# Adding gathered edge rows on VectorE instead of TensorE in a graph network

## The chip, the cores and the metric

The kernel runs on one core of one Trainium2 chip. The metric is the device time of one execution in microseconds (us). Five engines work side by side: TensorE (matrix products; PE, and PEld for loading its weights), VectorE (DVE), ScalarE (ACT), GpSimd (POOL) and SyncE (SP). Each has an instruction queue of its own that it works off in order. SBUF is the on-chip memory, PSUM the small memory into which TensorE writes; tables lie in DRAM. A gather is one indirect DMA on the POOL queue: for each of 128 partitions it fetches one row of a table, by a row number that lies in SBUF.

## What is computed

N = 6250 nodes carry 256 features, E = 100000 edges (src, dst) are sorted by dst. Each layer adds to each node the rows of the sources of its edges, and sends the result through three dense products:

```python
def agg(h):
    return jax.ops.segment_sum(h[src], dst, num_segments=N)
for l in range(NL - 1):          # NL = 4: three such layers
    h = x + agg(x)
    h = jax.nn.relu(h @ W1s[l] + b1s[l])
    h = jax.nn.relu(h @ W2s[l] + b2s[l])
    x = h @ W3s[l] + b3s[l]
h = x + agg(x)                   # and the last, with cW1, cW2 (64 wide), cW3
```

Before the first layer stand a layer norm and a relu; at the end the input is added. A node has 16 edges on average, and the number differs from node to node.

## The kernel before

The 6250 nodes are 49 blocks of 128. The kernel multiplies by the first weight before it aggregates, so what is gathered or multiplied is already a table of 256 columns for each layer (`tables`, one in DRAM for each layer). It aggregates in two ways at once.

*Panels.* For 31 of the blocks (`panels`), the adjacency matrix is built in layer 0 from one-hot products (`build`, L1013, with `one_hot`, L991, on VectorE and the casts L1043 and L1045), stored as bytes in DRAM (`mats`), and in every layer fetched again, cast to float (L1464 on ScalarE, L1466 on VectorE from layer 1 on) and multiplied with the whole table, which lies in SBUF as a high and a low part (`XY`). These are the products of L1491, 49 steps for each panel of up to four blocks. Layer 0 does not multiply the last panel, since it is still being built.

*Gathers.* The other blocks (`gone`: 22 in layer 0, 18 in each later layer) are gathered (class `Gathered`, L1264). The edges of a block's two halves of 64 nodes are taken in runs of 128, nine runs for each half, so 18 gathers (L1309) a block. A gathered tile holds 128 edges in edge order, so a row may belong to any node of the half. To add it up, VectorE makes a one-hot of 32 columns for each run (`one_hots`, L1334), and TensorE multiplies one-hot and rows into PSUM (`sums`, L1353). Runs that can touch two quarters take part twice: 22 products a block, in two visits, four of them side by side on different columns. Then VectorE adds the block's own row (L1371, L1380), TensorE transposes (L1391) and the block goes through the other products (`mlp`, L1169).

The order of all work is written out by the program, in one order for each engine. A model clock (`clock`, advanced by `passed` by the expected time of each product) stands for TensorE's progress. `Gathered.begin` spreads a layer's gathers evenly over the time that `work_of` expects for the layer, `send` puts each in the POOL queue behind the product then current (`after`), and rows are used LEAD = 21 us after they are asked for. A layer's gathers begin once its whole table is in DRAM (`store`, L1233). `tick` and `job` place the smaller steps.

*Preparation.* `look` (L607) finds where each node group's edges begin and fetches edge numbers in small gathers (`ask`, L597), while `normed` (L819) makes the first table. The first gathers of layer 0 go out as the matrix build starts; the first 28 steps only build (PRE), then products and build go on together.

Of the kernel before, what the change touches and what calls it, by code (L numbers as in the profile page):

```python
# [8 lines left out]
F32 = mybir.dt.float32  # L9
# [387 lines left out]
def sorted_edges(  # L397
# [56 lines left out]
    Q = P // 4  # L454
    TS = 9
    T = 2 * TS
    CUT = (3, 5)

    ROUNDS = [(3, 3), (4, 4), (0, 5), (1, 6), (2, 7), (None, 8)]
# [12 lines left out]
    S0 = 2 * panels[0][0]  # L472
    assert gone[-2] == panels[-1] and sorted(
        b + i for b, n in gone[:-2] + gone[-1:] + panels for i in range(n)) == list(range(NT))
    NQ = len(gone)
    PW = 4 * T

    left = [T * sum(n for _, n in gone[:q]) for q in range(NQ + 1)]

# [7 lines left out]
    clT = const.tile([P, 2, GSUB, NSUB - S0], BF16, name="clT")  # L487
    cT, loT = clT[:, 0], clT[:, 1]
    idx = const.tile([P, left[NQ]], I32, name="idx")
    rel = const.tile([P, left[NQ]], F32, name="rel")  # L490
# [7 lines left out]
    tables = [dram.tile([N, C], F32, name=f"table{l}") for l in range(NLAYER + 1)]  # L498
# [108 lines left out]
    def look(pool):  # L607
# [23 lines left out]
        nc.vector.memset(one, 1.0)  # L631
        firsts = pool.tile([1, EB], F32, name="near", bufs=1)
# [24 lines left out]

        place_i = pool.tile([P, NQ, PW], I32, name="hi", bufs=1)
        for q, (b, _) in enumerate(gone):
            nc.gpsimd.iota(place_i[:, q, :], pattern=[[1, PW]], base=T * b, channel_multiplier=-TS)  # L660
        place = pool.tile([P, 1], F32, name="place", bufs=1)
        nc.gpsimd.iota(place, pattern=[[0, 1]], base=0, channel_multiplier=P,
                       allow_small_or_imprecise_dtypes=True)
        node = pool.tile([P, GSUB], F32, name="node", bufs=1)
# [26 lines left out]
        for q in range(GSUB):  # L691
            for w, e in ((wd, dst), (ws, src)):
# [4 lines left out]
        both = pool.tile([P, 2], F32, name="both", bufs=1)  # L697
        sel = pool.tile([P, NQ, PW], F32, name="near_i", bufs=1)
        some = pool.tile([P, NQ, PW], F32, name="rel", bufs=1)
        nc.vector.tensor_copy(both[:NSUB, 0:1], first[:NSUB, 0:1])  # L700
        nc.vector.tensor_copy(both[:NSUB, 1:2], low[:NSUB])
        nc.vector.tensor_scalar(some[:NSUB], place_i[:NSUB], float(TS - 1), None, op0=OP.is_le)
        nc.vector.scalar_tensor_tensor(sel[:NSUB], place_i[:NSUB], 0.0, some[:NSUB],
                                       op0=OP.is_ge, op1=OP.mult)
        ps = ps_m.tile([P, W], F32, name="ps")
        for q in range(NQ):
            nc.tensor.matmul(ps[:PW, 2 * q:2 * q + 2], sel[:NSUB, q, :], both[:NSUB, :],
                             start=True, stop=True)
        spread = pool.tile([P, NQ, 2], F32, name="spread", bufs=1)
        nc.vector.tensor_copy(spread[:PW], ps[:PW, :2 * NQ].rearrange("p (q t) -> p q t", t=2))  # L710

        part = pool.tile([P, NQ], F32, name="part", bufs=1)
        nc.vector.scalar_tensor_tensor(part[:PW], spread[:PW, :, 1], float(-T), spread[:PW, :, 0],
                                       op0=OP.mult, op1=OP.add)
        for q, (b, _) in enumerate(gone):
            nc.vector.tensor_scalar(part[:PW, q:q + 1], part[:PW, q:q + 1], place[:PW, 0:1],
                                    float(T * P * b), op0=OP.add, op1=OP.add)
        skip = pool.tile([P, NQ], F32, name="skip", bufs=1)  # L720
        nc.vector.tensor_scalar(skip[:PW], part[:PW], float(E - P), None, op0=OP.min)
        from_i = pool.tile([P, NQ], I32, name="from_i", bufs=1)
        nc.vector.tensor_copy(from_i[:PW], skip[:PW])
        nc.vector.tensor_tensor(skip[:PW], part[:PW], skip[:PW], OP.subtract)
        base = pool.tile([P, NQ], F32, name="base", bufs=1)
        nc.vector.tensor_scalar(base[:PW], spread[:PW, :, 1], -1.0, None, op0=OP.add)
        gds = pool.tile([P, 2, NQ, P], I32, name="near_i", bufs=1)
        gd, gs = gds[:, 0], gds[:, 1]
        for q, (_, n) in enumerate(gone):
            for w, e in ((gd, dst), (gs, src)):  # L730
                asks.append((w[:n * T, q, :], e, from_i[:n * T, q:q + 1]))
# [3 lines left out]
        H = GSUB // 4  # L735
        for q0 in range(0, GSUB, H):
            cut = slice(q0, q0 + H)
            ask(len(asks) - 2 * (GSUB - q0 - H) - 2 * NQ)
            r = pool.tile([P, H, P], F32, name="rel", bufs=1)
            f = pool.tile([P, H, P], F32, name="f", bufs=1)  # L740
# [10 lines left out]
            for t, o in ((r, cT), (f, loT)):  # L751
                for i in range(0, H, 4):
                    ps = ps_m.tile([P, W], F32, name="ps")
                    for k in range(4):
                        nc.tensor.transpose(ps[:, k * NSUB:(k + 1) * NSUB], t[:NSUB, i + k, :],
                                            ident[:NSUB, :NSUB])
                    nc.scalar.copy(o[:, q0 + i:q0 + i + 4, :],
                                   ps[:, :4 * NSUB].rearrange("p (q s) -> p q s", q=4)[:, :, S0:])
            yield

# [859 lines left out]
```

## Time and profile before

| | us |
|---|---|
| median of three runs | 2344.69 (2342.46 to 2354.30) |
| the profiled execution, in all | 2343.82 |
| its span, first to last instruction | 2342.0 |
| TensorE busy | 2175.8 |
| VectorE busy | 972.8 |
| ScalarE busy | 891.8 |
| POOL busy | 1429.4 |

The granted TensorE clock was 0.98 over the span. The DMA engines were busy about half the time and moved 371 MB, 182 MB of it by the POOL queue. In the rows below, "L1309 POOL DMA_INDIRECT rows<-table,idx x1368 | 1374.1, 1004 | 830.7" means: line 1309, on POOL, an indirect DMA that writes the tile `rows`, 1368 times, 1374.1 us busy in all, 1004 ns on average, and 830.7 us of idle time of that engine just before them; what ended the idle time follows. In a row in order of time, the first two numbers are start and duration, and the brackets hold the idle time before it and what released it. Matmuls overlap, so a mean duration is longer than busy time divided by count; two records stand for one full float32 product.

### The profile page before, as it was taken

The page shows a single profiled execution, that of the slowest core. Times are in us where ns is not written, and L with a number is a line of the kernel's source. Part 1 is how long each engine was busy: PE and PEld are TensorE (multiplying, and loading weights), DVE is VectorE, ACT ScalarE, POOL GpSimd, SP SyncE. Part 2 cuts the span into 40 slices and gives each one's busy share as a digit, 9 for nine tenths or more (in the row PEclk, how much of TensorE's full clock was granted, in tenths as well). Part 3 has the DMA queues.
Part 4 walks back from the last instruction along what each step waited for, and adds up shares of the span by engine and source line. Part 5 has one row for each costly group of instructions (what it writes and reads, how often), then busy time and mean ns, then how long its engine had stood idle before and what let it go on. Part 6 is the DMA issues. An engine that isn't in the chain of part 4 may idle for free. (4 is left out here: it accounts for less than half of the span.)

```text
span 2342.0 us, 34300 instructions
## 1 busy us (share of the span) xinstructions
PE 2175.8 (93%) x12062; PEld 1570.0 (67%) x12062; DVE 972.8 (42%) x2844; ACT 891.8 (38%) x1816; POOL 1429.4 (61%) x1442
## 2 busy tenths in 40 slices
PE   5888998999998999999999999999999999999898
PEld 3656666666665877676766877777677866666565
DVE  6887656556555422222223422222224423232222
ACT  4775545454545423232223432232233322222221
POOL 3635666666666266666666366666664566666663
PEclk9979999999999999999999999999999999999999
DMA  4545555555556554444455554545445655545553
GB/s 151 152 154 176 173 158 174 159 166 173 164 173 200 165 151 151 149 131 149 148 156 178 181 152 134 170 136 161 140 152 159 182 167 156 168 143 172 158 153 107
DMA packets 195882, 371.43 MB, mean 159 GB/s; under 512 B 32790, under 2 KB 122986, under 8 KB 195700
## 3 DMA queue, kind: packets, MB, share of 16 engines
q0 software_dynamic: 67264, 181.96, 26.9%
q1 hardware_dynamic: 126510, 185.34, 24.2%
q8 instruction: 96, 1.57, 0.3%
q10 hardware_dynamic: 1926, 1.85, 0.3%
q14 instruction: 86, 0.70, 0.1%
HBM read 310.61 MB, written 58.07 MB: 157 GB/s over the span
## 5 line engine op out<-in xcount | busy, mean ns | idle before, releaser
L1309 POOL DMA_INDIRECT rows<-table,idx x1368 | 1374.1, 1004 | 830.7 <-PE agg L1491 276.0
L1491 PE MATMUL agg<-a,XY 128*128 128x512 f32 (+1 forms) x6076 | 1484.3, 394 | 52.6 <-issue 39.0
L1491 PEld LDWEIGHTS agg<-a,XY 128*128 128x128 f32 x6076 | 1108.4, 189 | 334.6 <-issue 126.0
L1464 ACT CAST a<-at 128x512 fp32r<-128x512 uint8 (+1 forms) x943 | 546.9, 607 | 694.7 <-PE agg L1491 528.9
L1466 DVE CAST a<-at 128x512 fp32r<-128x512 uint8 (+1 forms) x576 | 256.2, 459 | 582.2 <-PE agg L1491 397.8
L1353 PE MATMUL sums<-rows,hot 128*32 128x256 f32 x3344 | 240.4, 387 | 8.1 <-issue 4.4
L1043 ACT CAST at<-bp 128x392 uint8<-128x392 f32 x276 | 131.3, 488 | 277.8 <-PE bp L1035 197.4
L1045 DVE CAST at<-bp 128x392 uint8<-128x392 f32 x220 | 124.1, 564 | 218.2 <-PE bp L1035 152.3
L1353 PEld LDWEIGHTS sums<-rows,hot 128*32 128x32 f32 x3344 | 106.0, 110 | 132.1 <-issue 72.2
L1035 PE MATMUL bp<-hi,lo 128*128 128x196 bf16 x992 | 143.7, 264 | 47.3 <-issue 18.7
L1035 PEld LDWEIGHTS <-lo 128*128 128x128 bf16 x992 | 76.0, 102 | 129.4 <-issue 86.6
L1380 DVE TENSOR_TENSOR u<-u,sums 128x256 f32<-128x256 f32 x76 | 31.8, 419 | 309.4 <-PE agg L1491 301.4
L1183 PE MATMUL ps<-h,w 128*128 128x512 f32 (+5 forms) x392 | 158.3, 544 | 0.5 <-issue 0.5
L994 DVE TENSOR_TENSOR hi<-cols,pairs 128x784 bf16<-128x784 bf16 x248 | 139.3, 562 | 0.0
L1212 PE MATMUL ps<-w,h 128*128 128x256 f32 x588 | 134.8, 380 | 3.4 <-PE ps L1212 1.6
L1334 DVE TENSOR_TENSOR hot<-colf,rel 128x64 f32<-128x64 f32 x836 | 126.9, 220 | 0.0
L1212 PEld LDWEIGHTS ps<-w,h 128*128 128x128 f32 x588 | 110.5, 190 | 20.2 <-issue 2.7
L1183 PEld LDWEIGHTS ps<-h,w 128*128 128x128 f32 (+1 forms) x392 | 67.2, 184 | 65.3 <-issue 56.4
L1230 DVE TENSOR_TENSOR zz<-ps,w 128x512 f32<-128x512 f32 (+1 forms) x78 | 50.2, 658 | 137.8 <-PE ps L1212 82.3
L994 DVE TENSOR_TENSOR lo<-lanes,pairs 128x512 bf16<-128x512 bf16 x248 | 104.2, 420 | 2.6 <-ACT pairs L989 1.4
L1186 ACT ACTIVATE h<-ps,bias 128x512 f32<-128x512 f32 (+5 forms) x98 | 60.6, 634 | 114.1 <-PE ps L1183 81.6
L1398 ACT ACTIVATE h<-ps,bias 128x256 f32<-128x256 f32 (+1 forms) x84 | 33.5, 450 | 149.4 <-PE agg L1491 48.8
(138 smaller groups left out, 744.9 us busy)
## 6 DMA issues: line engine op xcount, KB each, us to landing
at<-mat SPq DMA_DIRECT2D x189, 448.0 KB
mat<-at SPq DMA_DIRECT2D x31, 784.0 KB
rows<-table,idx POOLq DMA_INDIRECT x1368
table<-zz SPq DMA_DIRECT2D x69, 256.0 KB
back<-table SPq DMA_DIRECT2D x118, 128.0 KB
at<-mat SPq DMA_DIRECT2D x25, 336.0 KB
xs<-in_x_dram SPq DMA_DIRECT2D x8, 768.0 KB
table<-zs SPq DMA_DIRECT2D x24, 256.0 KB
```

Of the source, the lines that this page charges most:

```text
L994: nc.vector.tensor_tensor(o.rearrange("p q (n t) -> p q n t", t=2), values.rearrange("p (n t) -> p n t", t=2)[:, None, :, :].to_broadcast( ...
L1035: mm = nc.tensor.matmul(bp[:, m * HW:(m + 1) * HW], lo[:, q + m, :], hi[:, q + m, :], start=True, stop=True)
L1043: nc.scalar.copy(o, v)
L1045: nc.vector.tensor_copy(o, v)
L1183: mm = nc.tensor.matmul(ps[:mp, :w], weights[l][0][:, c, i * P:i * P + mp], h1[:, c, :w], start=(c == 0), stop=(c == KC - 1))
L1212: mm = nc.tensor.matmul(o, h2[0][:, c, nodes], w3[:, c, :], start=(c == 0), stop=(c == KC - 1))
L1309: got = nc.gpsimd.indirect_dma_start(out=t, out_offset=None, in_=tables[self.l][:, :], in_offset=bass.IndirectOffsetOnAxis(ap=idx[:, o:o + ...
L1334: nc.vector.tensor_tensor(hot[:, i, :, :], colf[:, None, i * Q:(i + 1) * Q].to_broadcast([P, 2, Q]), rel[:, o + k:o + k + TS + 1:TS, None] ...
L1353: nc.tensor.matmul(self.sums[(2 * h + m) * Q:(2 * h + m + 1) * Q, :C], self.hots[r, m][:, h, :], self.rows[g, h, k], start=(r == 0), stop= ...
L1464: nc.scalar.copy(o, mat[l, p][j])
L1466: nc.vector.tensor_copy(o, mat[l, p][j])
L1491: mm = nc.tensor.matmul(agg[c][:, :w], XY[:, j, o:o + P], a[:, :w], start=(j == 0 and half == 0), stop=(j == NT - 1 and half == 1))
```

## The change

Gathered rows come by node instead of by edge. Tile k of a block holds, in partition p, the row of node p's k-th edge, for k below K = 17; a node with fewer edges gets a row of zeros (the tables have 128 rows more, filled with zeros). Such tiles need no one-hot: VectorE adds them up. Two tiles share a buffer of 128x512, so one add handles a pair (`pair`, seven for a block), and `fold` adds both halves, the 17th tile and the block's own row. Edges beyond a node's 17th go into OV = 2 further tiles of 128 slots for the whole block, which pass two full one-hot products on TensorE (`add`). A block has 19 gathers instead of 18, TensorE two products instead of 22.

```diff
+            def pair(self, g, k):
+                t = self.rows.pop((g, k))
+                if k == 3:
+                    self.acc = work.tile([P, 2, C], F32, name="acc", bufs=1)
+                    nc.vector.tensor_tensor(self.acc, self.rows.pop((g, 1)), t, OP.add)
+                else:
+                    nc.vector.tensor_tensor(self.acc, self.acc, t, OP.add)
+            def fold(self, g):
...
+                nc.vector.tensor_tensor(u, XY[:, b, :C].bitcast(F32), XY[:, b, C:].bitcast(F32),
+                                        OP.add)
...
+                nc.vector.tensor_tensor(u, u, self.acc[:, 0, :], OP.add)
+                nc.vector.tensor_tensor(u, u, self.acc[:, 1, :], OP.add)
+                nc.vector.tensor_tensor(u, u, self.rows.pop((g, K - 1)), OP.add)
+                self.hot = work.tile([P, OV, P], F32, name="hot", bufs=2)
+                nc.vector.tensor_tensor(self.hot, colf[:, None, :].to_broadcast([P, OV, P]),
+                                        rel[:, c, :, None].to_broadcast([P, OV, P]), OP.is_equal)
+            def add(self, g):
+                b, n, i, _ = self.blocks[g]
+                for j in range(OV):
+                    mm = nc.tensor.matmul(sums[:, :C], self.hot[:, j, :], self.rows.pop((g, K + j)),
+                                          start=(j == 0), stop=(j == OV - 1))
+                    passed(C * FULL32, mm)
+                self.finish(b, n, i, sums)
```

The pace follows the new counts, and rows are used 13 us after they are asked for. The buffers are seven pairs and four single tiles instead of 24 to 26 single ones. The model clock's price for two visits a block (VISIT) goes, `work_of` counts two products.

```diff
             def begin(self):
                 self.first = clock[0] + LEAD
                 self.end = begun[self.l] + work_of(self.l) - TAIL
-                self.pace = (self.end - self.first) / (self.upto[-1] - self.upto[1])
+                self.pace = (self.end - self.first) / (len(self.order) - 1)
...
-        LEAD, TAIL = 21.0, 10.0
-        COLS, FULL32, TURN, VISIT, BUILD, BURST = 0.457e-3, 1.68e-3, 0.4, 1.7, 0.2, 0.3
+        LEAD, TAIL = 13.0, 10.0
+        COLS, FULL32, TURN, BUILD, BURST = 0.457e-3, 1.68e-3, 0.4, 0.2, 0.3
...
-            t += len(layers[l].blocks) * (sum(VISIT for _ in VISITS[l > 0]) + TURN)
+            t += len(layers[l].blocks) * (OV * C * FULL32 + TURN)
```

In the preparation, `look` no longer fetches runs of 128 edges for the gathered blocks (14 small gathers) and turns them by transposes (L800). It counts where each single node's edges begin (`count`, small comparisons and products of one column), brings the counts to the nodes' partitions by products, and gathers the first 17 edge numbers of every node, one small gather for each of the 22 blocks. Where a node has fewer, `slot_rows` puts the number of a zero row. Two blocks ahead of their use in layer 0, `overflow` finds the edges beyond the 17th with a comparison and two small products and gathers their numbers, two more small gathers a block, in the POOL queue between the row gathers. Layer 0's row gathers begin after 22 of the 56 steps that only build, instead of before the first. The build has two PSUM buffers instead of three, since `overflow` takes one.

```diff
+        for c in range(NG):
+            asks.append((idx[:, c, :], src, from_i[:, c:c + 1]))
         ask(len(asks))
...
+        def gather():
+            for j in range(OV):
+                asks.append((over[:, c, j:j + 1], src, e_i[:, j:j + 1]))
+            ask(OV)
+
+        later(1, edges)
+        later(3, gather)
...
-        ) as ps_a, tc.tile_pool(name="ps_b", bufs=3, space=PSUM) as ps_b:
+        ) as ps_a, tc.tile_pool(name="ps_b", bufs=2, space=PSUM) as ps_b:
             begun = {0: clock[0]}
-            layers[0].begin()
-            layers[0].send(layers[0].upto[1])
+            READY = 22
...
+                if built[0] == READY:
+                    slot_rows()
+                    layers[0].begin()
```

Some steps may no longer follow each other closely: after a step of the dense products, adds and transposes of a gathered block are held back for one or two steps (`held`).

More of the change, by code (lines that the diff above doesn't have):

```diff
@@ L694, in look @@
         ask(4)
[L697 to L731, printed above, removed]
         yield
         H = GSUB // 4
+        begins = pool.tile([P, GSUB + 1, GD], F32, name="begins", bufs=1)
@@ L796, in look @@
[L796 to L806 removed]
+        count(GSUB - H)
@@ L1090, in job @@
             jobs.append((now[0] + first, now[0] + last, fn))
-        queue = []
+        queue, ahead = [], []
         def step(visit):
@@ L1102, in step @@
             free[0] = now[0] + (2 if g["hurry"] else 4)
+            held[0] = now[0] + (1 if g["hurry"] else 2)
             if g["steps"]:
@@ L1117, in tick @@
                 first, last, fn = task
-                if first <= now[0] and (visit or last <= now[0]):
+                if max(first, held[0]) <= now[0] and (visit or last <= now[0]):
                     jobs.remove(task)
```

319 lines of the change are left out of this document (192 added, 127 removed).

## The prediction

> **What bounds the kernel now.** I read the page's busy shares and the chain of waits first, then the groups by line, then the layers one by one.
>
> ```profile
> PE 2175.8 (93%) x12062; PEld 1570.0 (67%) x12062; DVE 972.8 (42%) x2844; ACT 891.8 (38%) x1816; POOL 1429.4 (61%) x1442
> by line: PE agg L1491 32.1%; PE sums L1353 4.9%; PE ps L1183 3.2%; PE ps L1212 2.3%; issue 1.7%; PE ps L1209 1.1%; another core or an unknown queue 0.4%; PE ps L1391 0.3%; DMA back<-table 0.1%; ACT h L1398 0.1%; ACT a L1464 0.0%; ACT h L118
> ```
>
> TensorE is busy 93% of the span and makes up nearly all of the chain that the profile could follow; the sums of gathered rows (L1353) are its second largest piece. A mean over the span hides the layers, so here are the four (layer 0 from its first steady gather; each later one from its first gather to the next layer's, the last to the end). Columns: PE, PEld, DVE, ACT and POOL busy.
>
> ```profile
> 159.40:760.50 601.10, 549.07 (x3468) 376.78 (x3466) 367.92 (x1010) 311.64 (x685) 401.98 (x388) 0.99 0.56 172
> 798.90:1314.30 515.40, 501.89 (x2700) 373.81 (x2699) 157.26 (x500) 163.03 (x309) 320.68 (x324) 1.00 0.51 156
> 1314.30:1829.10 514.80, 501.85 (x2705) 374.66 (x2704) 155.60 (x499) 162.27 (x309) 320.54 (x324) 1.00 0.51 155
> 1829.10:2342.00 512.90, 472.59 (x2505) 335.20 (x2503) 155.04 (x487) 136.37 (x249) 321.71 (x324) 0.97 0.51 157
> ```
>
> In layers 1 and 2 TensorE has 13 us idle of 515. But POOL's 321 us is less idle than it looks: consecutive gathers show what a gather costs its queue.
>
> ```profile
> 1282.22 0.96 POOL L1309 DMA_INDIRECT rows<-table,idx  x1 [0.30 <-issue]
> 1314.34 0.95 POOL L1309 DMA_INDIRECT rows<-table,idx  x1 [31.16 <-DMA w<-in_L_gnn_W2s_dram]
> 1315.60 0.95 POOL L1309 DMA_INDIRECT rows<-table,idx  x1 [0.30 <-PE agg L1491]
> 1316.86 0.95 POOL L1309 DMA_INDIRECT rows<-table,idx  x1 [0.31 <-issue]
> 759.48 0.95 POOL L1309 DMA_INDIRECT rows<-table,idx  x1 [0.30 <-issue]
> 798.93 1.19 POOL L1309 DMA_INDIRECT rows<-table,idx  x1 [38.50 <-ACT a L1464]
> 2311.83 0.95 POOL L1309 DMA_INDIRECT rows<-table,idx  x1 [0.30 <-issue]
> 762.34 0.62 PE L1353 MATMUL sums<-rows,hot 128*32 128x256 f32 x2 [0.66 <-DMA rows<-table,idx]
> 1286.50 1.50 PE L1353 MATMUL sums<-rows,hot 128*32 128x256 f32 x20
> ```
>
> A gather takes 0.95 us and 0.30 us always follow: 1.26 us from start to start at best. Gathers fill 798.9 to 1283.2 in layer 1, 484 us for 324, one in 1.49 us. A layer has 31 to 39 us without gathers, in which the new table is finished. At the end of layer 0 TensorE already waits for rows (the row at 762.34): POOL is close behind TensorE as the bound.
>
> **The change, part by part.**
>
> ```profile
> L1353 PE MATMUL sums<-rows,hot 128*32 128x256 f32 x3344 | 240.4, 387 | 8.1 <-issue 4.4 <-DMA rows<-table,idx 2.3 <-DVE hot L1334 0.7
> L1212 PE MATMUL ps<-w,h 128*128 128x256 f32 x588 | 134.8, 380 | 3.4 <-PE ps L1212 1.6 <-ACT h L1398 1.5 <-issue 0.3
> L1334 DVE TENSOR_TENSOR hot<-colf,rel 128x64 f32<-128x64 f32 x836 | 126.9, 220 | 0.0
> L1202 DVE TENSOR_TENSOR xt<-xt,cb3r 128x512 f32<-128x512 f32 (+1 forms) x24 | 14.7, 652 | 2.2 <-DMA xt<-in_x_dram 2.2
> L1371 DVE TENSOR_TENSOR u<-XY 128x256 f32<-128x256 f32 x76 | 31.8, 419 | 0.0
> ```
>
> *TensorE.* A node block loses 44 matmul records, 240.4/76 = 3.16 us. It gets two full f32 products of 256 columns, two records each; L1212 is that form, 134.8/588 = 0.229 us a record, so 0.92 us. That frees 2.24 us a block: 49 us in layer 0 (22 blocks), 40 us in each later layer (18). TensorE alone would then need 475 us a layer.
>
> *VectorE.* A block gets seven adds of 128x512 (14.7/24 = 0.61 us of busy time each), three more of 128x256 (0.42) and one one-hot of 256 columns (0.42 by the same row); it loses eleven one-hots (126.9/76 = 1.67 us). Net 4.27 + 1.26 + 0.42 - 1.67 = 4.3 us a block, 326 us in all: VectorE goes from 42% to about 57%. As work this is hidden by its idle time; I cost it at nothing, except for what it does to the gathers. Each add waits for its rows in VectorE's order, with the casts of the next matrix tiles queued behind it, and TensorE waits for those; with the lead now 13 instead of 21 us, late rows become TensorE's wait.
>
> *POOL, rows.* A block takes 19 gathers instead of 18: 418 in layer 0, 342 in each later one. Layer 0 also gets two small gathers of edge numbers for each block (44), in the same queue. I price them as a row gather.
>
> *POOL, price of a gather.* Here the trace of before gives bounds. The first rows are layer 0's and layer 1's gathers as groups, then two gathers 2 us apart with the VectorE work beside them, one of layer 0, and the VectorE groups that matter (the rows with x192, x198, x42 and x18 are layer 1's alone).
>
> ```profile
> L1309 POOL DMA_INDIRECT rows<-table,idx x388 | 402.0, 1036 | 218.1 <-issue 75.7 <-PE bp L1035 64.4 <-PE agg L1491 58.0
> L1309 POOL DMA_INDIRECT rows<-table,idx x324 | 320.7, 990 | 202.1 <-PE agg L1491 74.8 <-issue 60.8 <-ACT a L1464 38.5
> 1071.91 0.42 DVE L1371 TENSOR_TENSOR u<-XY 128x256 f32<-128x256 f32 x1
> 1071.97 1.52 POOL L1309 DMA_INDIRECT rows<-table,idx  x1 [0.30 <-issue]
> 1073.62 0.69 DVE L1230 TENSOR_TENSOR zz<-ps,w 128x512 f32<-128x512 f32 x1 [0.95 <-PE ps L1212]
> 1073.79 0.95 POOL L1309 DMA_INDIRECT rows<-table,idx  x1 [0.30 <-PE ps L1212]
> 354.66 2.13 POOL L1309 DMA_INDIRECT rows<-table,idx  x1 [0.30 <-issue]
> L994 DVE TENSOR_TENSOR hi<-cols,pairs 128x784 bf16<-128x784 bf16 x248 | 139.3, 562 | 0.0
> L994 DVE TENSOR_TENSOR lo<-lanes,pairs 128x512 bf16<-128x512 bf16 x248 | 104.2, 420 | 2.6 <-ACT pairs L989 1.4 <-issue 0.3
> L1466 DVE CAST a<-at 128x512 fp32r<-128x512 uint8 (+1 forms) x192 | 86.0, 460 | 189.0 <-PE agg L1491 140.5 <-issue 17.1 <-remote 16.5
> L1334 DVE TENSOR_TENSOR hot<-colf,rel 128x64 f32<-128x64 f32 x198 | 30.1, 220 | 0.0
> L1131 DVE TENSOR_TENSOR XY<-back,XY 128x256 fp32r<-128x256 f32 x42 | 16.8, 420 | 10.1 <-ACT XY L1130 8.3 <-issue 0.9 <-DMA back<-table 0.9
> L1371 DVE TENSOR_TENSOR u<-XY 128x256 f32<-128x256 f32 x18 | 7.5, 418 | 0.0
> ```
>
> A gather that starts beside an add that reads two tiles of SBUF takes 1.52 us; one beside an add that reads PSUM takes 0.95. In layer 0, where a run of such instructions stood, one took 2.13. The new adds are all of the first kind. Over layer 1 the mean gather is 0.04 us above 0.95, while casts (86 us) and the two-tile instructions below them (54 us) cover 27% of the layer. The change raises that cover by about 19 points (6.4 us a block of 25.5, less the 1.9 of the old ones), with adds half as long again: I take 0.08, so 0.95 + 0.08 + 0.30 = 1.33 us. In layer 0 the mean is 0.086 above with L994 alone covering 243 of 601 us; the cover grows by about half, so 0.13, and 1.38 us. Ends: 1.26 (no gather is ever held; a gain below that is excluded by the row at 1316.86) and, when every gather that meets an add loses a whole 0.65 us and runs form in layer 0, 1.43 and 1.48.
>
> [...]
>
> *Preparation.* Gathering the 22 blocks' edge lists replaces 14 small gathers, and they can only be asked for after the last count.
>
> ```profile
> 107.02 0.91 POOL L601 DMA_INDIRECT near_i<-in_src_dram,from_i  x1 [0.30 <-issue]
> 120.53 0.95 PE L800 MATMUL ps<-ident,wd 72*128 72x72 f32 x7
> 129.50 0.50 PE L1035 MATMUL bp<-hi,lo 128*128 128x196 bf16 x4 [1.80 <-DVE hi L994]
> 158.21 1.65 PE L1491 MATMUL agg<-a,XY 128*128 128x384 f32 x4 [0.92 <-ACT a L1464]
> ```
>
> The step that stood at 120.5 (L800) is where the new requests start, 22 of about 1.25 us, to about 150. The matrix build starts at 129.5, and 22 builds of 56 in 28.7 us bring it to about 141; there VectorE must wait for the lists, some 10 to 13 us, with the build's one-hots behind it. Nothing hides that: the first products start at about 170 instead of 158. (The other new preparation work about equals what it replaces; bounds -5 and +10 us. One build buffer less in PSUM costs nothing while POOL sets the pace; without that cover I would add up to 10 us.) By the kernel's own clock about six rows go out before that point.
>
> *The sum.* Layer 0: from 170 there are 412 rows and about 40 small gathers, 452 x 1.38 = 624 us, so the last ends at 794; layer 1's gathers come 38.5 us later (the distance after 759.48, when rows were late too), at 832 instead of 798.9: **+33**. TensorE's 49 us don't show. Layers 1 to 3: 342 x 1.33 = 455 us, and about 30 us without gathers: after the last gather lands, the last sums start (1286.50) and the next layer's gathers come 28 us later. That is 485 instead of 515.4 and 514.8; the last, with 29 us from its last gather to the end, 484 instead of 512.9: -30, -30, -29. Above TensorE's 475, so POOL sets them. Sum: 33 - 89 = **-56** on a span of 2342.0. The profiled execution took 2343.8 us in all, within 0.1% of the median of the three runs, 2344.7: I predict **2288 us**.
>
> **The rivals.**
>
> *The gathers keep their price* (1.34 and 1.29 us, their means of before plus 0.30). Layers 1 to 3 then need 441 + 30 = 471, so TensorE's 475 rules: -40, -40, -38. Layer 0: 170 + 452 x 1.34 + 38.5 = 814, +15. Together -103: 2241. For it: layer 1's mean is only 0.04 us above an undisturbed gather. Against: the 1.52 us row. 0.20.
>
> *TensorE sets everything*, if lists come early and the small gathers are cheap: layer 0 also gives 49 less the 12 of preparation: 2343.8 - 118 - 37 = 2189. Against: 452 gathers at even 1.26 us fill 570 us. 0.05.
>
> *Late rows hold up VectorE*, whose casts then come late for TensorE on top of the gathers' own time. If each of the 54 blocks of layers 1 to 3 costs TensorE one pair of casts (2 x 0.46 us): 50 us, 2338. For it: VectorE's order is fixed. Against: five steps of the product are prepared ahead (AHEAD + 2). 0.10.
>
> *Slower: gathers and adds meet in runs* on VectorE, the fold's four adds and one-hot above all, and a gather waits for the whole run, as at 354.66. With both layers' kinds at one period p the span is 170 + 38.5 + 89 + 1478 p (452 + 3 x 342 gathers), which is 2342 at p = 1.38 us; this decides from there. At 1.43 and 1.48 it is 297.5 + 1467 + 669 = 2434. For it: 1.38 is only 0.05 above my mean. Against: VectorE would be idle over 40% of the time, so most adds stand alone. 0.17, spread from 2340 to 2434.
>
> *My forecast*, POOL sets all layers at little over its old price: 0.48, own range 2255 to 2325.
>
> **How the numbers follow.** 0.5% is 12 us, about what a measurement of this kernel can tell from no change (its three runs span 2342.5 to 2354.3). Faster: forecast 0.46, first rival 0.20, second 0.05, a part of the third 0.04: 0.75. Slower: most of the last rival, 0.15. Same: 0.10. The range 2225 to 2345 leaves out the second rival and most of the slower one, and takes in the low end of the gathers' price in layers 1 to 3.
>
> **What would show it.** Right: two records pairs for each block in place of 44 under the sums line; POOL the engine with back-to-back gathers through whole layers, mean near 1.08 us in layer 0 and 1.03 later; TensorE's share down to about 88%, with waits that lead through VectorE's adds to gathered rows; layer 1's first gather at about 830, then every 485 us. Wrong: a mean gather of 0.99 us or less with TensorE above 97% in layers 1 to 3 (first rival), or 1.13 us and more (slower). If the first products start near 158, my preparation step fails. If POOL shows gaps over 1 us inside a layer that is long, something else than its own pace held it.

## The result: 195 us slower, and the profile after

The changed kernel took 2539.9 us (median of four runs, 2534.1 to 2541.9) against 2344.6 us: a ratio of 1.082, 95% interval 1.0785 to 1.0855. I had forecast 2288 us. Later, in three rounds, it was 2510.1 against 2318.5 us: 1.081 (1.0774 to 1.0845). Whatever the kernel, in some runs (those just named, and the experiments e1 to e4, e13, e18) TensorE's completion signals reach the other engines up to 11 us late, in others (e5 to e12, e14 to e17) within 0.4 us, and times are compared only among runs of one sort. Without late signals the kernel before takes 2173 to 2178 us and the changed kernel 2293, in single runs: 118 us slower.

First the page of the changed kernel: its first part, TensorE's clock over 40 slices, and the group of the main products. Below it stand the clock and the main products of the kernel before.

```profile
PE 2149.9 (85%) x9093; PEld 1603.5 (63%) x9093; DVE 1315.5 (52%) x2939; ACT 896.4 (35%) x1812; POOL 1588.1 (63%) x1574
...
PEclk9959998988898899999999999999999999899898
...
L1565 PE MATMUL agg<-a,XY 128*128 128x512 f32 (+1 forms) x6076 | 1612.1, 415 | 121.7 <-issue 74.8
```

```profile
PEclk9979999999999999999999999999999999999999
L1491 PE MATMUL agg<-a,XY 128*128 128x512 f32 (+1 forms) x6076 | 1484.3, 394 | 52.6 <-issue 39.0
```

VectorE rose from 42% to 52%, so it is not full. POOL rose from 61% to 63%, but the 0.30 us after each gather are not in that share, so it has to be looked at more closely. TensorE fell from 93% to 85%, with the product groups' time up from 1484.3 to 1612.1 us for the same 6076 records and the idle time before them from 52.6 to 121.7. The clock row shows where the longer records come from: 8s in many slices where the page of before has 9s, and 0.92 over the span instead of 0.98; a 128x512 record within a stretch at half clock took 0.63 us in the median, one at full clock 0.40.

By stage, in rows of one stretch each (from, to, length, then busy time of TensorE, its weight loads, VectorE, ScalarE and POOL, the granted clock, the DMA share and GB/s): the kernel before's four layers, each from its first product to the next layer's, then the changed kernel's.

```profile
158.20:779.70 621.50, 567.20 (x3537) 389.66 (x3537) 370.87 (x1017) 319.40 (x703) 401.98 (x388) 0.99 0.54 167
779.70:1298.20 518.50, 504.14 (x2712) 375.74 (x2713) 159.93 (x504) 165.04 (x314) 320.68 (x324) 1.00 0.51 156
1298.20:1813.20 515.00, 502.05 (x2706) 374.87 (x2705) 155.80 (x499) 162.47 (x309) 320.54 (x324) 1.00 0.51 155
1813.20:2342.00 528.80, 488.49 (x2581) 348.67 (x2579) 164.26 (x507) 144.48 (x268) 321.71 (x324) 0.97 0.51 156
```

```profile
190.50:898.80 708.30, 566.87 (x2694) 413.46 (x2694) 477.03 (x1093) 323.30 (x703) 463.63 (x451) 0.91 0.49 151
898.80:1439.20 540.40, 487.89 (x1981) 374.60 (x1982) 236.68 (x502) 163.42 (x311) 348.66 (x342) 0.96 0.50 154
1439.20:1980.60 541.40, 495.23 (x1986) 377.85 (x1984) 234.64 (x498) 161.73 (x309) 347.55 (x342) 0.95 0.50 152
1980.60:2532.20 551.60, 484.24 (x1871) 354.17 (x1869) 242.71 (x508) 146.70 (x271) 351.70 (x342) 0.91 0.50 154
```

The 190 us of the span: preparation +32 (first product 158.2 to 190.5), layer 0 +87, then +22, +26 and +23. TensorE is busy for less time in layers 1 to 3 (487.9 after 504.1 in layer 1) and yet they are longer.

My forecast said that POOL would run without a gap through layers 1 to 3. Its gathers in layer 1, by what they fetch (count, busy time, mean, and the idle time just before them, 0.30 us of which belongs to every gather):

```profile
L1391 POOL DMA_INDIRECT rows<-table,idx x288 | 293.2, 1018 | 169.2 <-issue 52.6 <-ACT a L1538 44.1 <-PE agg L1565 35.3
L1391 POOL DMA_INDIRECT last<-table,over x36 | 36.7, 1020 | 19.4 <-issue 5.9 <-PE ps L1289 4.9 <-PE agg L1565 3.1
L1391 POOL DMA_INDIRECT last<-table,idx x18 | 18.8, 1042 | 8.6 <-issue 2.7 <-PE ps L1466 2.6 <-remote 1.8
```

342 gathers took 348.7 us and 342 x 0.30 = 103 us of issue: 451 us, where I had 455. But they are spread over 501.8 us. POOL idled about 50 us, and it was not the bound.

What it waited for is seen best at one place. TensorE, ScalarE and POOL in the changed kernel, in order of time:

```profile
1067.64 10.85 PE L1565 MATMUL agg<-a,XY 128*128 128x512 f32 x45
1078.81 1.09 PE L1565 MATMUL agg<-a,XY 128*128 128x512 f32 x3 [0.32 <-issue]
1086.31 2.08 PE L1565 MATMUL agg<-a,XY 128*128 128x512 f32 x4 [6.41 <-ACT a L1538]
```

```profile
1084.49 1.27 ACT L1581 ACTIVATE h<-agg,bias 128x512 f32<-128x512 f32 x2 [12.09 <-remote]
1085.64 1.66 ACT L1538 CAST a<-at 128x512 fp32r<-128x512 uint8 x3
```

```profile
1080.71 0.96 POOL L1391 DMA_INDIRECT last<-table,idx  x1 [0.30 <-issue]
1084.72 0.96 POOL L1391 DMA_INDIRECT last<-table,over  x1 [3.05 <-remote]
```

All product records are in the trace (31 panels of 196), so a panel's last one can be counted off: this panel's ended at 1073.6, within the first row. ScalarE's read of that panel (h<-agg) waits for it and began at 1084.49, 10.9 us later, after 12.09 us of idle time. The casts of the next steps stand behind it in ScalarE's order, so TensorE, which had gone on with the next panel, ran out of them at 1079.9 and stood for 6.4 us; POOL's next gather, which waits for a signal of TensorE, stood for 3 us. In the kernel before these reads came at most 4.0 us after the last product. My first reading of this trace was the third rival in a larger form, since VectorE's adds also show idle time that ends with gathered rows: adds wait for rows, casts stand behind adds, TensorE starves. The first experiments were made for that.

### The profile page after: what moved, and what is told of

It is laid out like the page before. It is cut to its first block, busy times and chain, and to the rows that moved or that the text cites. A ratio compares the mean times of both kernels' runs of the same rounds, so it can differ in the third digit from the quotient of the medians.

```text
span 2532.2 us, 29316 instructions
## 1 busy us (share of the span) xinstructions
PE 2149.9 (85%) x9093; PEld 1603.5 (63%) x9093; DVE 1315.5 (52%) x2939; ACT 896.4 (35%) x1812; POOL 1588.1 (63%) x1574
## 5 line engine op out<-in xcount | busy, mean ns | idle before, releaser
L1565 PE MATMUL agg<-a,XY 128*128 128x512 f32 (+1 forms) x6076 | 1612.1, 415 | 121.7 <-issue 74.8
L1391 POOL DMA_INDIRECT rows<-table,idx x1216 | 1237.7, 1018 | 681.8 <-issue 220.6
L1565 PEld LDWEIGHTS agg<-a,XY 128*128 128x128 f32 x6076 | 1173.2, 200 | 418.3 <-issue 136.4
L1419 DVE TENSOR_TENSOR acc<-acc,rows 128x512 f32<-128x512 f32 x456 | 313.0, 686 | 34.2 <-DMA rows<-table,idx 23.1
L1108 PE MATMUL bp<-hi,lo 128*128 128x196 bf16 x992 | 154.9, 272 | 139.8 <-issue 49.3
L1108 PEld LDWEIGHTS <-lo 128*128 128x128 bf16 x992 | 84.9, 104 | 219.1 <-issue 155.8
L1391 POOL DMA_INDIRECT last<-table,over x152 | 159.6, 1050 | 75.4 <-issue 25.4
L1289 PE MATMUL ps<-w,h 128*128 128x256 f32 x588 | 142.2, 388 | 17.7 <-ACT h L1473 6.3
L1445 PE MATMUL sums<-last,hot 128*128 128x256 f32 x304 | 85.7, 405 | 27.7 <-DVE hot L1439 18.1
L1391 POOL DMA_INDIRECT last<-table,idx x76 | 80.8, 1063 | 38.6 <-issue 13.8
```

The lines of the kernel that those rows point to most:

```text
L1108: mm = nc.tensor.matmul(bp[:, m * HW:(m + 1) * HW], lo[:, q + m, :], hi[:, q + m, :], start=True, stop=True)
L1289: mm = nc.tensor.matmul(o, h2[0][:, c, nodes], w3[:, c, :], start=(c == 0), stop=(c == KC - 1))
L1391: got = nc.gpsimd.indirect_dma_start(out=t, out_offset=None, in_=tables[self.l][:, :], in_offset=bass.IndirectOffsetOnAxis(ap=at, axis=0),)
L1419: nc.vector.tensor_tensor(self.acc, self.acc, t, OP.add)
L1445: mm = nc.tensor.matmul(sums[:, :C], self.hot[:, j, :], self.rows.pop((g, K + j)), start=(j == 0), stop=(j == OV - 1))
L1565: mm = nc.tensor.matmul(agg[c][:, :w], XY[:, j, o:o + P], a[:, :w], start=(j == 0 and half == 0), stop=(j == NT - 1 and half == 1))
```

## The experiments

**e1: the adds' wait taken away.** The adds stay, but the sums lack the gathered rows.

```diff
-  nc.vector.tensor_tensor(self.acc, self.acc, t, OP.add)
+  nc.vector.tensor_tensor(four(self.acc), four(self.acc), still, OP.add)   # still: a constant tile; likewise the first pair and the last row
```

> The gathers, their pace and the number, size and place of VectorE's adds stay as in the changed kernel, but the pair adds and the fold read a constant tile in place of the gathered rows (the sums of the first 17 rows are left out of the output). So the adds' work stays and their wait for rows goes. If the wait is what costs (VectorE stands before a late row, casts queue behind it, TensorE runs dry and then pays windows at half clock): layers 1 to 3 fall from 541/542/530 us to 475 to 495 each, TensorE's idle time before the products to about 50 us, the whole to 2330 to 2400. If the adds' own work costs (VectorE's time or its traffic in SBUF): layers 1 to 3 stay within 10 us of 541, the whole above 2500. If late completion signals of TensorE cost by themselves: also unchanged, and ScalarE's evacuations still come up to 10 us after the last product of a panel.

2525.1 us; layer 1 540.1 us. **e2: the adds left out**, and with them the first 17 rows of each sum.

> The pair adds and the fold's three adds of rows are left out altogether (the sums of the first 17 rows are missing in the output); gathers, one-hot products and everything else stay. Wait theory: the same as with constant operands, 2330 to 2400. Work theory: 2330 to 2400 here, but not there. Signal theory: no change, above 2500. What this kernel gains beyond the one with constant operands is the price of the adds' work; I expect under 15 us.

2533.4 us. The stretch of layer 1, and the gathers in it:

```profile
893.60:1436.20 542.60, 486.37 (x1980) 375.37 (x1981) 137.53 (x322) 162.16 (x311) 334.24 (x342) 0.96 0.49 153
```

```profile
L1391 POOL DMA_INDIRECT rows<-table,idx x288 | 281.4, 977 | 181.5 <-issue 60.7 <-PE agg L1560 54.2 <-ACT a L1533 42.6
```

VectorE is busy for 137.5 us instead of 236.7, no instruction of it waits for the first 17 rows of a block, and the layer takes 542.6 us against 540.4. A gather takes 0.977 instead of 1.018 us; POOL has 14 us less to do (334.2 instead of 348.7), and it only idles 14 us longer. The adds, as work and as a wait, cost nothing here, and neither does POOL's own work set the length of this layer. **e3: VectorE's half of the casts moved to ScalarE**, and **e4: more lead:**

```diff
-  if l == 0 or j % 2 == 0:
+  if True:
```

> In layers 1 to 3 the half of the casts that VectorE makes goes to ScalarE, so that no cast stands behind an add. Wait theory: most of the loss of these layers goes (each 485 to 505 us, the whole 2400 to 2470; layer 0 is as before, its casts were on ScalarE already). Work or signal theory: no gain; ScalarE, with about 110 us more work a layer, may become a little worse, 2530 to 2580.

```diff
-  LEAD, TAIL = 13.0, 10.0
+  LEADS, TAIL = (13.0, 20.0), 10.0     # layer 0, the others
-  name="rows", bufs=7    name="last", bufs=4
+  name="rows", bufs=9    name="last", bufs=5     # layers 1 to 3
```

> In layers 1 to 3 the gathers run 20 instead of 13 us of the kernel's own clock ahead of the adds, with 9 pair buffers and 5 single ones in place of 7 and 4 (the room comes from one buffer of the inputs at the very end). Wait theory: rows have landed when VectorE comes to them; layers 1 to 3 fall to 480 to 505 us, the whole to 2410 to 2470. Work or signal theory: no change beyond 10 us.

2524.5 and 2541.4 us, layer 1 538.7 and 545.4. Four edits at four links of that chain, and no layer from 1 to 3 moved by more than 5 us: the theory is dead. What was left was the late signal itself.

**e5 and e6: fewer signals of TensorE**, in the changed kernel and in the one before.

```diff
-  passed(2 * w * COLS, mm)
+  passed(2 * w * COLS, mm if c else None)    # gathers are tied to a step's second product only
```

> The adds are out of it: without them, without their wait, without casts behind them or with more lead the time stayed. What is left is that ScalarE's evacuation at a panel's end came up to 10.9 us after the last product (before: up to 4.0), and that TensorE's completion signals often come 0.71 us apart or a multiple of it while it streams products. Signal theory: about 1.3 signals a step are more than TensorE gets out in the 0.93 us of a step. Here a gather is paced by the second product of a step alone, whose signal the casts need anyway, not by the first as well: some 140 of 626 signals a layer go. By that theory layers 1 to 3 fall from 541/542/530 us to 480 to 510, the whole to 2420 to 2480. If it is something else (the gathers' place, the form of the sums, the order of the steps): within 10 us of 2540.

> The same edit in the kernel before. Signal theory: its evacuations wait less too; up to 40 us faster, 2300 to 2345. Something else: no change, 2340 to 2350.

2293.0 and 2176.0 us, beside 2174.6 us for the kernel before: these runs met no late signals, so they say nothing on the theory, and together with **e9**, the changed kernel as it is, only that the edit is worth nothing there.

> The changed kernel once more, unchanged. The last four kernels ran on a chip on which the kernel before took 2175 us instead of 2350 and TensorE's completion signals came at once (evacuations within 0.05 us of a panel's last product). Theory: on such a chip POOL alone sets the changed kernel (gathers back to back, 1.30 us each in layers 1 to 3, 1.37 in layer 0) and it takes 2285 to 2300; where the signals come late, 2530 to 2550, with POOL idle some 48 us a layer although the gathers' price is the same.

2293.0 us, as expected. The gathers of layer 1 in e9, and the stretches of its layers:

```profile
L1391 POOL DMA_INDIRECT rows<-table,idx x288 | 287.1, 997 | 129.4 <-ACT a L1538 41.9 <-PE agg L1565 34.1 <-issue 32.6
L1391 POOL DMA_INDIRECT last<-table,over x36 | 35.9, 997 | 11.0 <-issue 3.7 <-PE agg L1565 3.4 <-DVE acc L1419 2.7
L1391 POOL DMA_INDIRECT last<-table,idx x18 | 17.5, 970 | 5.5 <-DVE acc L1419 1.5 <-PE agg L1565 1.5 <-PE ps L1289 0.9
```

```profile
185.00:823.70 638.70, 545.50 (x2695) 394.34 (x2695) 474.13 (x1093) 324.42 (x703) 473.42 (x451) 0.94 0.54 168
823.70:1305.60 481.90, 463.86 (x1981) 367.25 (x1981) 233.52 (x502) 166.65 (x311) 340.39 (x342) 0.99 0.55 173
1305.60:1793.20 487.60, 469.42 (x1986) 370.22 (x1985) 233.07 (x498) 165.63 (x309) 343.09 (x342) 0.98 0.54 169
1793.20:2291.20 498.00, 453.60 (x1871) 344.10 (x1869) 239.57 (x508) 148.76 (x271) 342.99 (x342) 0.97 0.55 170
```

342 gathers with 340.5 us of work now take 444.4 us from the first to the last: 340.5 + 103, with no gap left. So here POOL does set layers 1 to 3, at 1.30 us a gather. For the kernel before without late signals stands **e12**, the edit of e6 once more:

> The kernel before with a gather paced by the second product of a step alone (479 instead of 608 signals in layer 1). Where signals come late and their rate counts: layers 1 to 3 from 519/515/521 us to 495 to 505, the whole from 2344 to 2260 to 2310. Where they come at once: no change, 2170 to 2180, as it was on such a chip.

```profile
149.80:709.70 559.90, 552.13 (x3537) 385.53 (x3537) 370.23 (x1017) 323.48 (x703) 403.69 (x388) 0.99 0.59 186
709.70:1207.30 497.60, 496.75 (x2711) 376.58 (x2712) 162.49 (x504) 167.40 (x314) 314.76 (x324) 1.00 0.52 163
1207.30:1701.20 493.90, 493.90 (x2708) 374.11 (x2706) 159.89 (x499) 165.49 (x309) 314.55 (x324) 1.00 0.52 162
1701.20:2175.80 474.60, 466.00 (x2581) 345.98 (x2579) 166.90 (x507) 147.86 (x268) 318.76 (x324) 0.99 0.55 174
```

```profile
L1309 POOL DMA_INDIRECT rows<-table,idx x324 | 314.8, 971 | 186.6 <-PE agg L1491 85.2 <-issue 52.1 <-ACT a L1464 40.1
```

2177.6 us, beside 2174.2 for the kernel before. TensorE is busy for 496.75 of 497.6 us and 493.9 of 493.9: it is the bound of layers 1 and 2. POOL's row is that of layer 1; of its 186.6 us, 40.1 are the way from layer 0 and 97 the 0.30 us of each gather, so 49 are left. The change takes 33 and 24 us of work from it, POOL with its 18 more gathers stops the layers at 482 and 488, and the gain is 16 and 6 us. Layer 3 had less for TensorE to do (466 us) and comes out 23 us longer, 18 x 1.30. Layer 0 is 79 us longer: 460 gathers at 1.38 us fill 633 us.

**e15: POOL's work cut**, by leaving out rows beyond the 17th (their lists, gathers and products).

> The changed kernel without rows beyond the 17th: their lists, their gathers and the one-hot products are left out (the output lacks those rows). POOL's work falls from 460 to 374 gathers in layer 0 and from 342 to 306 in each later one; adds, casts and the rest stay. Where TensorE's signals come at once: POOL sets the changed kernel there (460 x 1.38 = 635 us in layer 0, 342 x 1.31 + 38 = 486 later), so layer 0's gathers fall to about 515 to 550 us, layers 1 to 3 to 465 to 480, where TensorE's own work takes over, and the whole from 2293 to 2130 to 2190. Where they come late: POOL now has 40 to 50 us a layer to spare, as in the kernel before, so layers 1 to 3 fall from 541/542/530 to 490 to 510 and the whole to 2290 to 2360; if the late signals cost through casts and buffers instead, to 525 or more, the whole above 2420.

2061.0 us, better than I had expected, again without late signals. Its layers 1 and 2, and its gathers in layer 1:

```profile
720.50:1163.10 442.60, 441.75 (x1908) 351.80 (x1909) 226.72 (x466) 165.11 (x311) 313.91 (x306) 1.00 0.56 177
1163.10:1605.40 442.30, 442.30 (x1913) 352.57 (x1912) 223.07 (x462) 164.24 (x309) 310.40 (x306) 1.00 0.56 175
```

```profile
L1394 POOL DMA_INDIRECT rows<-table,idx x288 | 296.3, 1029 | 128.1 <-ACT a L1527 40.0 <-issue 39.3 <-PE agg L1554 31.5
```

36 gathers fewer, 39 us less in layer 1 (481.9 to 442.6), with all pair adds in place: POOL's bound is shown by taking work from it (TensorE loses the products too and VectorE 7 us of one-hots, but neither was full in e9). TensorE is busy for 441.8 of 442.6 us now, so both end together. Layer 0 goes from 638.7 to 539.5 us with 86 requests fewer (the last gathers of that layer start at 698.8 instead of 800.2).

**e8: layer 0's start and its third buffer.**

```diff
-  from_i = pool.tile([P, NG], I32, name="from_i", bufs=1)
+  from_i = const.tile([P, NG], I32, name="from_i")
-  READY = 22
+  READY = 44
-  ps = ps_g.tile([P, W], F32, name="pt")              name="ps_b", bufs=2
+  ps = sums[:, C:]                                    name="ps_b", bufs=3
```

> Layer 0 alone: the tile with the edge lists' positions is kept apart so that the matrix build need not wait for the lists, VectorE asks for the lists after 44 builds instead of 22, and the build gets its third buffer in PSUM back (the small products share the bank of the sums). First products at 158 to 165 instead of 190.5; panels of layer 0 at 92 to 97 us instead of 94 to 109 if the third buffer covers late signals there; layers 1 to 3 as they are; the whole 2440 to 2500. If the buffer doesn't matter, only the start comes back: 2505 to 2520.

2273.1 us, to be held against e9's 2293.0: 20 us. VectorE at the start of the build in the changed kernel, then in e8:

```profile
154.94 0.43 DVE L1067 TENSOR_TENSOR lo<-lanes,pairs 128x512 bf16<-128x512 bf16 x1 [23.11 <-ACT pairs L1062]
```

```profile
128.32 0.42 DVE L1067 TENSOR_TENSOR lo<-lanes,pairs 128x512 bf16<-128x512 bf16 x1 [1.85 <-ACT pairs L1062]
```

The changed kernel's build did not begin at all until the edge lists had landed; with the tile of their positions kept apart it begins at 128.3 instead of e9's 149.5, and the first products come at 160.6 instead of 185.0. From there layer 0 took 641.3 us, against 638.7: the third buffer brought nothing, while POOL idles for only some 7 us of the 625 that e8's gathers in this layer take, beyond the 0.30 of each.

**e11, e13: fewer signals and e8's edits together.**

> The changed kernel with both earlier edits: a gather is paced by the second product of a step alone (502 instead of 626 signals of TensorE in layer 1, 500 of 615 and 474 of 609 in the others), and layer 0 gets its early build and its third buffer. Where signals come late: layers of both kernels took 0.82 (layer 0) to 0.89 us for each signal of TensorE there (760 signals in 620 us and 849 in 707, 608 in 519 and 626 in 540). If the rate of signals sets the time, layers 1 to 3 fall to about 485 each (then POOL's own pace, 342 x 1.32 + 35), and the whole to 2300 to 2400. If each late signal is another accident, and their number doesn't matter: layers 1 to 3 stay at 530 to 541, the whole 2490 to 2520. Where signals come at once: as with the early build alone, 2260 to 2275.

2266.8 us, without late signals, as expected for that case. The same kernel met them in e13:

> The kernel of the last study with both edits once more, in the hope of a chip on which TensorE's signals come late (the kernel before takes about 2345 us there). If the number of signals sets the time there: layers 1 to 3 about 485 us each instead of 541/542/530, the whole 2300 to 2400. If not: layers 1 to 3 at 530 to 541, the whole 2490 to 2520. On a chip where they come at once: 2260 to 2275 again.

2500.1 us, beside 2317.0 for the kernel before. Its layer 1, and for comparison that of the unchanged kernel in **e18** (2510.1 us on the same chip; the expectation of e18 gave 2530 to 2550 and was 20 to 40 too high):

> The changed kernel unchanged, against the kernel before in three rounds on one chip. Where TensorE's signals come at once, 2285 to 2300 us against 2172 to 2180, a ratio of 1.050 to 1.058; where they come late, 2530 to 2550 against 2315 to 2355, 1.075 to 1.10.

```profile
881.70:1417.30 535.60, 487.78 (x1981) 375.04 (x1982) 237.31 (x502) 162.70 (x311) 348.24 (x342) 0.96 0.50 155
```

```profile
887.90:1423.10 535.20, 485.19 (x1980) 375.68 (x1981) 237.68 (x502) 163.98 (x311) 347.70 (x342) 0.95 0.50 155
```

535.6 and 535.2 us with 502 and 626 signals: the number of signals is not it either. The 12 us between the two profiled executions (2498.2 and 2510.5) lie before the first product, which comes at 176.5 and 188.9.

**e10, e14, e16, e17: no pacing wait**, alone (e10, e16, e17) and with e8's edits (e14).

```diff
-  after(got, "rows are asked for evenly over a layer")
```

> The changed kernel, but a gather no longer waits for the product that it was tied to; it waits only for its buffer. Pacing theory: where TensorE's signals come late, POOL, which has hardly any time to spare, idles for them and never makes it up; without the wait layers 1 to 3 fall from 541/542/530 to 485 to 510 us, the whole to 2380 to 2450. Where the signals come at once: POOL had no gap to lose, so within 15 us of the changed kernel. Rival: the late signals cost through the casts (TensorE waits for ScalarE and VectorE, which wait for TensorE's signal that a buffer is free): then no gain on either, within 15 us.

> The changed kernel without the pacing wait of the gathers (they wait for their buffers alone) and with the early build and third buffer of layer 0. Slack theory: where TensorE's signals come late, a layer in which POOL has no idle time loses 54 to 58 us (changed layers 1 to 3, and the kernel before's layer 3), one in which it has 47 us of idle loses 22 (the kernel before's layers 1 and 2), because a gather that waits for a late signal is never made up; POOL's idle time in the changed kernel is 40 to 50 us a layer there. Without the pacing wait layers 1 to 3 fall from 536 to 545 (with late signals) to 490 to 505, the whole to 2350 to 2400. Rival: the late signals hold the casts, TensorE and VectorE, and buffers come free late: layers 1 to 3 stay at 530 to 545, the whole 2480 to 2500. On a chip without late signals: 2255 to 2270.

> The changed kernel without the pacing wait of the gathers once more, in the hope of a chip with late signals (the kernel before at 2315 to 2350 there). Slack theory: POOL's gaps of 40 to 50 us a layer go, layers 1 to 3 fall from 541/542/530 to 490 to 505, the whole to 2400 to 2440. If the late signals cost through casts and buffers: POOL's gaps stay, the whole above 2500. On a chip without them 2285 to 2295, as before.

> As the last run, which met no late signals: with them, slack theory 2400 to 2440 and layers 1 to 3 at 490 to 505 us; casts and buffers above 2500; without them 2285 to 2295.

2287.3, 2269.9, 2288.9 and 2293.4 us. All four fell among runs without late signals, where POOL has no gap to lose; against e9's 2293.0 and e8's 2273.1 the wait costs 6 us at most. What it costs with late signals was never measured.

**e7: sums in quarters, made three times over.**

> The changed kernel with the two products of a block's sums cut into quarters of 32 columns and made three times over, with the same result: 48 short records a block, as many as before the change (44), so TensorE gets its old load back, about 2.2 us a block. If the short products were what let late signals through before (runs of signals 0.05 us apart came beside them), the delays go: the whole 2400 to 2500. If not: 2540 to 2650, as TensorE has 40 us a layer more to do.

2652.5 us, also without late signals, so its question stays unanswered; and the load was not the old one. A quarter product's record shows 0.38 us like a full one's, and layer 1 became 593 us long (893.1 to 1486.6), 112 more than e9's, or 6.2 us a block.

No kernel here that computes everything beats the kernel before.

## Why the prediction was wrong

**The step that failed** is in the sum: "342 x 1.33 = 455 us, and about 30 us without gathers ... Above TensorE's 475, so POOL sets them". With late signals POOL did not set them. The 455 were 451, but 50 us of POOL's idle time came on top in layer 1, and the sum put nothing there. I had taken the idle time in the row of before (202.1 us before 324 gathers; 97 of it are the 0.30 us of each, 38 the way from the layer before, about 66 the rest) for room that a fuller POOL would fill. Without late signals POOL idles 49 us in that layer, while TensorE is full; that is room, and the changed kernel does fill it. With late signals 50 us are idle although POOL has more to do, and in e2, where it has 14 less to do, 64 are. Some 30 of the 50 us end, by the profile, with a signal of TensorE, and for some 19 it names no engine. In the sum I set a POOL without late signals beside a kernel before with them. My 485 us for layers 1 and 2 are the 482 and 488 of e9, and my 2288 us are within 5 of its 2293, but the kernel before takes 2175 there.

**A term mis-sized, and luck:** without gathers a layer goes not 30 us but 40 (1420.4 to 1461.0, and 1286.2 to 1327.4 in e9). In e9 the gathers of a layer took 444 us for my 455, so two errors of 10 us cancel in the 485. Layer 1's gathers began there at 843 for my 832, and the last layer, from its first gather on, took 476 us for my 484. That the sum comes so near to e9 is in part luck.

**Layer 0.** The price was right: 1.38 us start to start in e9 as forecast, 460 requests in 633 us (451 of them from the first product on, in 616 us; I had 452 and 624). The working behind it had an error: L994's 243 us are those of the whole run, and 196 fall into the 601 us of layer 0. With late signals the same requests took 702 us (172.4 to 874.4), of which 92 were idle time beyond the 0.30. I had 33 us more than before for this layer and its preparation together; it was 119.

**Preparation.** First products at 170 were forecast, 190.5 measured (185.0 without late signals). I let 22 builds go in while the lists were on their way; none did. The build's first tiles waited until the lists that read their positions from the preparation's memory were through: with these positions kept apart, which is the edit of e8 that can move the first build, that build came 21 us sooner and the first products, with all edits of e8, 24.

**TensorE and VectorE.** TensorE's busy time in layer 1 fell by 33 us where nothing else disturbs it (496.75 to 463.86), for 40 forecast. VectorE's adds were costed at nothing but the gathers, and e1 and e2 bear that out; they lengthen a gather by 0.04 us or 4% in the mean (0.977 in e2 to 1.018), and the 1.018 stand beside my 1.03. Of the 1026 gathers of layers 1 to 3 in the changed kernel, 137 start during a pair add (L1419), with a median of 1.36 us; the 736 that overlap none of these adds have a median of 0.96. So the 1.52 us row shows what one gather beside an add took, not the mean.

**The rivals.** The third named casts that come late for TensorE, as they do at 1086.31, but adds that wait for rows as the cause, and that is wrong: e1 to e4. The slower one named the period at which it decides, 1.38 us; the periods were 1.47 and 1.53, but by idle time, not by gathers that met adds. My sentence that gaps over 1 us inside a long layer would mean something else than POOL's own pace was the right sign, and it showed.

**What stays open** is the rest of the loss where signals are late: preparation and POOL's 18 to 64 more requests a layer explain the 118 us that are lost without them, and about 75 more are not explained. Set side by side, late signals cost the kernel before 62, 21, 21 and 54 us in its four layers (621.5 against 559.9 and so on), the changed one 70, 59, 54 and 54. Two explanations stand, and no experiment decides between them, since the kernels without the pacing wait did not meet late signals.

The first is that POOL loses time to late signals and has none to make it up with. The six layers that lose 54 or more are those in which POOL has, without late signals, at most 19 us of idle time beyond the 0.30 us of each gather; the two that lose 21 have 49. But e2 speaks against it: POOL has 13 to 17 us less to do there in each of layers 1 to 3, and these layers are not shorter but 1 to 2 us longer.

The second is that late signals leave TensorE without casts, and that it then runs at a lower clock, as the last section shows. From the first product on, late signals add 102 us to TensorE's busy time in the changed kernel (1932.4 in e9, 2034.3) and 53 in the kernel before (2008.8 in e12, 2061.9); that is 49 more, of the 75 in question. Why TensorE should wait more often in the changed kernel is open too: the signals there came up to 10.9 us late at the end of a panel, in the kernel before up to 4.0, and no run tells why.

## What to carry to other kernels

An engine's idle time is room for more work only if you can say what each wait in it is for; a wait that all engines share comes along into the changed kernel. When a second engine is close to being the bound, work that is moved from the first to it is worth only the distance between them (here 16 and 6 us of 33 and 24), and layers in which the second was already the bound pay in full. And before a loss is laid to the new instructions, leave them out once.

## What the runs showed of the hardware

**Late signals.** At the end of a panel ScalarE's read began, in some runs, up to 11.1 us after the last product record (10.9 in the changed kernel's first profile, 11.1 in e3), in the others 0.17 us after it as a rule and never more than 0.4; one and the same chip gave both. In the runs with late signals the trace also holds only some 60% of the signals that ScalarE and VectorE gave (1053 of 1739 and 1610 of 2727 in the changed kernel) and 28% of the records of landed DMAs (9376, where e9 has 33701), so what ended a wait is less certain there; in the others it holds all of these engines' signals (of VectorE's 2727 in e9, 2727). TensorE's came in steps of 0.71 us: some 450 of the changed kernel's lie 0.7 to 0.8 us after the one before, some 40 of e5's. What makes them late, no run here shows.

**The clock after a short pause.** In these traces the granted clock falls to one half in windows of 3.41 us, and which ones can be told from the window before. In the changed kernel, of 55 windows at full clock in which TensorE was busy for less than half, 54 were followed by one at half clock; of 61 between 50 and 70%, 12; of 504 above 70%, none. Once at half clock, all 40 windows with TensorE busy for less than 80% were followed by another, and 8 of 73 above. From these counts I estimate that a stall of 2 us, more than half a window, can cost a window at half clock after it. From the first product on, the changed kernel had 63 stretches at half clock with 316 us in all and the kernel before 12 with 53; without late signals these were 28 with 149 (e9) and 3 with 18 (e12).
